# A graph network's first loop: ScalarE alone reads h from PSUM, GpSimd makes half of each row, and the order of the nodes is worked out in eight pieces

## The chip, the cores and the metric

The kernel runs on one core of a Trainium2 chip. Its time is the device time of one execution in microseconds (us), and lower is better. The core has five engines that each work through a queue of their own in order: PE (TensorE, matrix products into PSUM), DVE (VectorE), ACT (ScalarE), POOL (GpSimd) and SP (SyncE, which here only issues transfers). ACT and POOL issue transfers too, from the same queue as their arithmetic. An engine that waits for a semaphore holds up everything behind it in its queue.

## The reference

Four graph layers run one after the other on x, of shape 8 x 2048 x 64 (batch, nodes, features), each followed by a residual and a layer norm. The change lies in the first. Cut to what it touches:

```python
h = x @ W                                            # 8 x 2048 x 64
s = leaky_relu(h @ a_node, 0.2)
alpha = softmax(where(H.T > 0, s[:, None, :], NEG))  # over the nodes, for each of 64 hyperedges
agg = einsum('ben,bnf->bef', alpha, h)               # a weighted mean of h for each hyperedge
beta = sigmoid((h @ a_gn)[:, None, :] + (agg @ a_ge)[:, :, None])
all_he = beta[..., None] * h[:, None] + (1 - beta[..., None]) * agg[:, :, None]
# per node: elu(all_he), weighted over the hyperedges that the node belongs to
```

H says which node belongs to which of the 64 hyperedges; most nodes belong to few. The rest of the layer multiplies by the 2048 x 2048 matrix adj, as do the three layers after it.

## The kernel before

The 2048 nodes stand in NT = 16 groups of 128, one node of a group on each partition, and the loop over t (lines 597 to 645) takes one group per pass. In a pass PE makes h and the two scores h·a_node and h·a_gn for all 8 batches, four products into the PSUM tile ph (L600; two such tiles). DVE clips the scores into seen (L611) and makes the leaky ReLU lr (L618); ACT takes Exp of both (L616 into the row st, L622 into ex). From ph in PSUM, DVE then makes two things: the row st, (h + 1) times the first Exp, in two halves of 4 batches (L625), and ex, h times the second Exp (L629). PE adds ex into the sums of the hyperedges, pagg, with the mask m_n as weights (L637); this is called the gather here. POOL copies the group's slot numbers to the row's end (L614). A row tile holds two passes, there are three such tiles, and after every odd pass ACT issues the store of a pair to hs_hbm (L635, 584 KB).

Meanwhile SP loads x for eight passes ahead (L460). POOL loads blocks of adj (L211); five of them are paced by the loop: `behind` (L482) copies one number of seen so that the load's issue waits for that pass. In passes 9 and 11, `parts` splits a block of x into a high part (ACT, L167) and a low part (POOL, L168).

Later stages take the nodes in order of the number of their hyperedges. Their ranks are worked out ahead of the loop, from L503 to L532. `place`, called in pass 9, turns ranks into the table `order`: DVE finds each rank's tile and row (L558 to L567), two tables of matches (L568 to L575), and one large table ohq of 128 x 2048 comparisons (L578); PE multiplies them (L582, into po) and DVE writes order (L587, L589).

After the loop PE begins the products with adj (ug, L172), POOL fetches the stored rows in the new order (`fetch_rows`, L275) and then the rest of adj, and DVE works out the hyperedges' means from pagg (L674 to L681) and their scores. Products stand in a written order, and `fill` sets pieces of the adj products between the other steps. The tile framework orders instructions that are not pinned with `keep_in_program_order`, and it adds the waits.

Of the kernel before, what the change touches and what calls it, by code (L numbers as in the profile page):

```python
# [30 lines left out]
F32 = mybir.dt.float32  # L31
F32R = mybir.dt.float32r
BF16 = mybir.dt.bfloat16
# [3 lines left out]
AF = mybir.ActivationFunctionType  # L37
ALU = mybir.AluOpType
AX = mybir.AxisListType
# [17 lines left out]
def tile_gnn_fast(  # L57
# [24 lines left out]
    nc = tc.nc  # L82
    B, N, F = out.shape
    E = h_nt.shape[2]
# [14 lines left out]
    def cols(c, n=C):  # L99
        return slice(c * n, (c + 1) * n)  # L100
# [70 lines left out]
    def mm(*args, **kw):  # L171
        tc.keep_in_program_order(nc.tensor.matmul(*args, **kw))  # L172
# [166 lines left out]
    def parts(p, c):  # L339
        part[c] = split(va, xc.pop((p, c)), f"v{c}", 1, [P, JT, P], nc.gpsimd, p == 0)  # L340
# [94 lines left out]
    with tc.tile_pool(name="pa_ps", bufs=1, space=PSUM) as pps:  # L435
# [10 lines left out]
        m_n = pa.tile([P, NT, E], F32, name="m_n")  # L446
        nc.sync.dma_start(m_n, h_nt)

        m_en = pa.tile([P, 2 * HROW], F32, tag="st", name="m_en", bufs=3)[:, 0:2 * C]
        nc.scalar.dma_start(m_en, h_e2)  # L450
        xt = {}

        def fetch_xt(t):
# [86 lines left out]
        pcm = pph.tile([P, 2, C], F32, tag="ph", name="pcm", bufs=2)  # L540
        pcm = pcm.rearrange("p k (t e) -> p (k t) e", e=E)
        mt = so.tile([P, 2 * C], BF16, name="mt")
        nc.vector.tensor_scalar(mt, m_en, 0.0, None, op0=ALU.is_gt)
        for t in range(NT // 2):
            for k in range(2):
                r = slice(k * E, (k + 1) * E)
# [3 lines left out]
        slot = pa.tile([P, NT, E], BF16, name="slot")  # L550
        nc.vector.tensor_tensor(slot, pcm, m_n, ALU.mult)

        def place():

            tl = so.tile([P, NT], F32, name="tl")
            ge = so.tile([P, NT, NT], F32, name="ge")
            tc.keep_in_program_order(
                nc.vector.tensor_scalar(over[:, 0:NT], iota[:, 0:NT], float(P), -0.5, op0=ALU.mult, op1=ALU.add)  # L558
            )
            wide = [P, NT, NT]  # L560
            nc.vector.tensor_tensor(
                ge, rank[:, :, None].to_broadcast(wide), over[:, None, 0:NT].to_broadcast(wide), ALU.is_gt
            )
            nc.vector.tensor_reduce(tl, ge, AX.X, ALU.add)
            nc.vector.tensor_scalar(tl, tl, -1.0, None, op0=ALU.add)
            q = so.tile([P, NT], F32, name="q")
            nc.vector.scalar_tensor_tensor(q, tl, -float(P), rank, op0=ALU.mult, op1=ALU.add)  # L567
            nc.vector.tensor_tensor(  # L568
                ge, tl[:, :, None].to_broadcast(wide), iota[:, None, 0:NT].to_broadcast(wide), ALU.is_equal
            )  # L570
            val = so.tile([P, NT, 2, NT], BF16, name="val")
            nc.vector.tensor_tensor(
                val[:, :, 0, :], ge, iota[:, 0:NT, None].to_broadcast(wide), ALU.mult
            )
            nc.vector.tensor_scalar(val[:, :, 1, :], ge, row, None, op0=ALU.mult)  # L575
            po = pps.tile([P, 2, NT], F32, tag="sm", name="po", bufs=2)
            ohq = so.tile([P, NT, P], BF16, name="ohq")
            nc.vector.tensor_tensor(  # L578
                ohq, q[:, :, None].to_broadcast([P, NT, P]), iota[:, None, :].to_broadcast([P, NT, P]), ALU.is_equal
            )  # L580
            for t in range(NT):
                nc.tensor.matmul(  # L582
                    po.rearrange("p i t -> p (i t)"), lhsT=ohq[:, t, :],
                    rhs=val[:, t].rearrange("p i t -> p (i t)"), start=t == 0, stop=t == NT - 1,
                )
            olo = so.tile([P, NT], F32, name="olo")
            nc.vector.tensor_copy(olo, po[:, 1, :])  # L587

            nc.vector.scalar_tensor_tensor(order, olo, float(NT), po[:, 0, :], op0=ALU.mult, op1=ALU.add)  # L589
            so_scope.close()  # L590


        seen = pa.tile([P, NT, B, 2], F32, name="seen")

        pagg = pps.tile([P, C], F32, tag="agg", name="pagg", bufs=1)
        G = B // 2
        for t in range(NT):
            ph = pph.tile([P, 2, C], F32, tag="ph", name="ph", bufs=2)
            for p in range(NP):
                nc.tensor.matmul(  # L600
                    ph[:, p // 2, (p % 2) * 2 * (F + 2):(p % 2 + 1) * 2 * (F + 2)], lhsT=xt[t][:, p, :],
                    rhs=bd66.rearrange("p b f -> p (b f)"), start=True, stop=True,
                )
            fetch_xt(t + 2 * XB)
            hv = ph[:, :, 0:G * (F + 2)].rearrange("p k (g c) -> p k g c", c=F + 2)
            if t % 2 == 0:
                st2 = pa.tile([P, 2, HROW], F32, tag="st", name="st", bufs=3)
            st = st2[:, t % 2]
            ex = pa.tile([P, 2, G, F + 1], F32, tag="ex", name="ex", bufs=2)
            sv = seen[:, t].rearrange("p (k g) c -> p k g c", k=2)  # L610
            nc.vector.tensor_scalar(  # L611
                sv, hv[:, :, :, F:F + 2], CLIP, -CLIP, op0=ALU.min, op1=ALU.max
            )
            nc.gpsimd.tensor_copy(st[:, BF + 8:], slot[:, t, :])  # L614
            e_gn = st[:, BF:BF + 8]
            nc.scalar.activation(e_gn.rearrange("p (k g) -> p k g", k=2), sv[:, :, :, 1], AF.Exp)  # L616
            lr = pa.tile([P, B], F32, tag="lr", name="lr", bufs=2)
            nc.vector.scalar_tensor_tensor(  # L618
                lr, seen[:, t, :, 0], 0.2, seen[:, t, :, 0], op0=ALU.mult, op1=ALU.max
            )  # L620
            tc.keep_in_program_order(
                nc.scalar.activation(ex[:, :, :, F], lr.rearrange("p (k g) -> p k g", k=2), AF.Exp)  # L622
            )
            for k in range(2):
                nc.vector.scalar_tensor_tensor(  # L625
                    st[:, k * G * F:(k + 1) * G * F].rearrange("p (g f) -> p g f", f=F), hv[:, k, :, 0:F], 1.0,
                    e_gn[:, k * G:(k + 1) * G, None].to_broadcast([P, G, F]), op0=ALU.add, op1=ALU.mult,
                )
            nc.vector.tensor_tensor(  # L629
                ex[:, :, :, 0:F], hv[:, :, :, 0:F], ex[:, :, :, F:F + 1].to_broadcast([P, 2, G, F]), ALU.mult  # L630
            )
            if t == 9:
                place()
            if t % 2:
                nc.scalar.dma_start(hs_hbm.rearrange("(p t) c -> p t c", t=NT)[:, t - 1:t + 1, :], st2)  # L635
            for k in range(2):
                nc.tensor.matmul(  # L637
                    pagg[k * E:(k + 1) * E, 0:G * (F + 1)], lhsT=m_n[:, t, :], rhs=ex[:, k].rearrange("p g c -> p (g c)"),
                    start=t == 0, stop=t == NT - 1,
                )  # L640
            if t in paced:
                behind(seen[:, t, 0, 0:1])
                load_adj(paced[t], 0)
            if t in (9, 11):
                parts(0, (t - 9) // 2)
        nc.vector.tensor_reduce(
            wrong[:, 2:3], seen.rearrange("p t b c -> p (t b c)"), AX.X, ALU.max, apply_absolute_value=True
        )
# [1974 lines left out]
```

## Time and profile before

| | us |
|---|---|
| four runs | 1738.89, 1742.17, 1742.26, 1743.68 |
| median | 1742.21 |
| the profiled execution | 1740.05 |
| its span, first to last instruction | 1737.9 |

| engine | busy us | share of the span |
|---|---|---|
| PE | 1658.7 | 95% |
| DVE | 830.2 | 48% |
| ACT | 589.2 | 34% |
| POOL | 573.0 | 33% |

A line of the timeline reads: start and length in us, engine, line of the kernel, operation, output <- inputs, sizes (partitions x elements), how often, and in brackets the idle time before it with what ended it. Several instructions of one kind in a row are one line; its length runs from the first start to the last end. Instructions of one engine overlap by some 0.08 us, so that a start can lie before the end of the one ahead. DMA issues are shown at the engine's queue, as ACTq or SPq. The granted clock is the share of PE's full clock that the chip allowed. Times in the stages are counted from the start of the span.

### The profile page before, as it was taken

The numbers are of one execution on the slowest core, as the hardware profiler recorded it, in microseconds if no ns is written. First come the engines' busy times: TensorE is split into PE (matmuls) and PEld (weight loads), VectorE is DVE, ScalarE is ACT, GpSimd is POOL, SyncE is SP. The second block draws the span as 40 slices with busy tenths as digits, with TensorE's granted clock in tenths as the row PEclk, the third lists the DMA queues.
The fourth block names the chain that finished last, engine by engine and source line by source line (L and its number), as shares of the span: only waits on it lengthen the run. The fifth ranks groups of instructions, "written<-read, shape, count | busy, mean of one in ns | idle before, by whom it ended". The sixth has DMA issues, their size and how long they took to land. (4 is left out here: it accounts for less than half of the span.)

```text
span 1737.9 us, 27994 instructions
## 1 busy us (share of the span) xinstructions
PE 1658.7 (95%) x11196; PEld 1209.5 (70%) x11196; DVE 830.2 (48%) x1547; ACT 589.2 (34%) x1031; POOL 573.0 (33%) x515
## 2 busy tenths in 40 slices
PE   6888899999989999999999999999989999999996
PEld 4667666666664444468788878888767877878775
DVE  7679945678642221210127247777623433433332
ACT  1345633434321211112123267878512222212221
POOL 4578845556534444422023001323310200202001
PEclk9899999999999999999999999999999999999998
DMA  9743344444240000017344367675571111211111
GB/s 342 244 162 125 103 133 139 153 141 145 94 146 6 31 11 20 25 57 291 118 145 125 108 155 157 133 172 123 157 263 45 53 55 43 61 49 43 56 43 38
DMA packets 171181, 195.83 MB, mean 113 GB/s; under 512 B 71537, under 2 KB 116337, under 8 KB 169761
## 3 DMA queue, kind: packets, MB, share of 16 engines
q1 hardware_dynamic: 160096, 154.54, 30.1%
q0 software_dynamic: 8544, 30.68, 5.2%
q10 hardware_dynamic: 2400, 8.72, 1.4%
q8 instruction: 90, 1.47, 0.4%
q14 instruction: 51, 0.41, 0.1%
HBM read 126.72 MB, written 67.17 MB: 112 GB/s over the span
## 5 line engine op out<-in xcount | busy, mean ns | idle before, releaser
L172 PE MATMUL ua<-pt,xn 128*128 128x512 f32 x512 | 230.2, 592 | 1.4 <-DVE pt L1150 1.4
L172 PEld LDWEIGHTS ua<-pt,xn 128*128 128x128 f32 x512 | 96.9, 190 | 111.1 <-issue 104.0
L1514 DVE COPY w_half<-pw 128x512 f32<-128x512 f32 x160 | 109.8, 706 | 85.7 <-PE pw L172 85.0
L1510 ACT COPY w_half<-pw 128x1024 f32<-128x1024 f32 x128 | 129.8, 1014 | 56.8 <-PE pw L172 56.7
L172 PE MATMUL py<-w_half,xg 128*32 128x128 f32 x4096 | 141.8, 279 | 1.4 <-issue 1.4
L172 PE MATMUL u<-adj,v0h 128*128 128x512 f32 x384 | 134.4, 427 | 1.1 <-ACT h L1818 1.1
L172 PE MATMUL u<-adj_more,v2h 128*128 128x512 f32 x384 | 126.2, 407 | 0.0
L172 PE MATMUL u<-adj_more,v2l 128*128 128x512 f32 x384 | 124.5, 401 | 0.0
L172 PE MATMUL u<-adj,v0l 128*128 128x512 f32 x384 | 124.5, 402 | 0.0
L172 PEld LDWEIGHTS py<-w_half,xg 128*32 128x32 f32 x4096 | 111.1, 138 | 18.7 <-issue 1.8
L1156 POOL TENSOR_TENSOR acc<-acc,pt 128x512 f32<-128x512 f32 x60 | 76.4, 1274 | 104.3 <-DVE pt L1150 103.7
L172 PE MATMUL pw<-est,wst 64*128 64x256 f32 x1024 | 110.1, 318 | 0.4 <-ACT w_half L1510 0.4
L1150 DVE TENSOR_SCALAR pt<-pt 128x512 f32<-128x512 f32 x64 | 29.6, 463 | 152.9 <-ACT pt L1149 152.7
L172 PEld LDWEIGHTS pw<-est,wst 64*128 64x128 f32 x1024 | 82.6, 184 | 25.1 <-ACT w_half L1510 16.7
L1727 ACT CAST ar<-fcav 128x512 fp32r<-128x512 f32 x64 | 39.5, 618 | 166.2 <-DMA fcav<-in_adj_t 165.3
L1149 ACT ACTIVATE pt<-s 128x512 f32<-128x512 f32 x64 | 38.0, 598 | 164.7 <-PE s L172 164.7
L172 PE MATMUL u<-adj,v1h 128*128 128x512 f32 x288 | 93.7, 403 | 0.0
L172 PE MATMUL u<-adj_more,v3h 128*128 128x512 f32 x288 | 93.4, 403 | 0.0
L172 PE MATMUL u<-adj_more,v3l 128*128 128x512 f32 x288 | 93.3, 399 | 0.0
L1728 DVE SCALAR_TENSOR_TENSOR ar<-fcav,ar 128x512 f32<-128x512 f32 x64 | 44.6, 697 | 100.2 <-ACT ar L1727 100.2
L172 PE MATMUL u<-adj,v1l 128*128 128x512 f32 x288 | 92.0, 397 | 0.0
L1699 POOL TENSOR_TENSOR x<-x,rows 128x512 f32<-128x512 f32 x16 | 22.6, 1438 | 210.3 <-PE pt L175 128.5
(406 smaller groups left out, 3274.8 us busy)
## 6 DMA issues: line engine op xcount, KB each, us to landing
fcav<-in_adj_t SPq DMA_DIRECT2D x64, 256.0 KB, 2.9
u_hbm<-ut SPq DMA_DIRECT2D x48, 256.0 KB, 3.3
xg<-u_hbm SPq DMA_DIRECT2D x24, 512.0 KB, 6.9
adj<-in_adj_t POOLq DMA_DIRECT2D x16, 512.0 KB, 8.1
adj_more<-in_adj_t POOLq DMA_DIRECT2D x16, 512.0 KB, 9.2
adj_hbm<-adj_more SPq DMA_DIRECT2D x16, 512.0 KB, 6.4
x_hbm<-r SPq DMA_DIRECT2D x28, 256.0 KB, 2.6
hs_hbm<-st ACTq DMA_DIRECT2D x8, 584.0 KB, 3.5
```

Of the source, the lines that this page charges most:

```text
L172: tc.keep_in_program_order(nc.tensor.matmul(*args, **kw))
L1149: nc.scalar.activation(pt, s, AF.Exp)
L1150: nc.vector.tensor_scalar(pt, pt, 1.0, None, op0=ALU.max)
L1156: nc.gpsimd.tensor_tensor(accs[c], accs[c], pt, ALU.add)
L1510: pin(nc.scalar.copy(dst, pw.rearrange("p j o n -> p n (j o)")))
L1514: pin(copy(dst[:, :, 2 * j:2 * j + 2], bank.rearrange("p o n -> p n o")))
L1699: nc.gpsimd.tensor_tensor(xs, xs, b2.to_broadcast([P, JT, P]), ALU.add)
L1727: nc.scalar.copy(ar, seen_a)
L1728: nc.vector.scalar_tensor_tensor(ar.bitcast(F32), seen_a, 1.0, ar.bitcast(F32), op0=ALU.mult, op1=ALU.not_equal, accum_out=left[:, t, k:k ...
```

## The change

ACT copies h and the scores from PSUM to a new SBUF tile hv (two of them), and writes h + 1 of the second four batches straight into the row with an Identity and a bias. DVE's clip, its half of the row and ex now read hv. POOL multiplies the second half of the row in place by the first Exp. A row tile holds one pass, there are four, and ACT issues a store in every pass (292 KB). The gather of a pass is issued after h of the next. `place` is cut into eight pieces: DVE's steps after passes 4 to 9 (ohq in quarters), PE's product after pass 11, the writing of order after pass 13. Nearly all of the loop's instructions are pinned to the written order. The mask m_en comes in two loads and is compared in two halves. Outside the loop and its preparations one thing differs: of the steps on the hyperedges' means, DVE takes both halves of the ELU (L680, L681) ahead of where it took them, and ACT its copy het.

```diff
-        m_en = pa.tile([P, 2 * HROW], F32, tag="st", name="m_en", bufs=3)[:, 0:2 * C]
-        nc.scalar.dma_start(m_en, h_e2)
+        m_en = [pa.tile([P, HROW], F32, tag="st", name="m_en", bufs=4)[:, 0:C] for _ in range(2)]
+        for i in range(2):
+            nc.scalar.dma_start(m_en[i], h_e2[:, cols(i)])
...
-        nc.vector.tensor_scalar(mt, m_en, 0.0, None, op0=ALU.is_gt)
+        for i in range(2):
+            nc.vector.tensor_scalar(mt[:, cols(i)], m_en[i], 0.0, None, op0=ALU.is_gt)
...
+        def row_columns(i):
+            r, quarter = slice(i * NT // 4, (i + 1) * NT // 4), [P, NT // 4, P]
+            hold(nc.vector.tensor_tensor(
+                ohq[:, r, :], q[:, r, None].to_broadcast(quarter), iota[:, None, :].to_broadcast(quarter),
+                ALU.is_equal,
+            ))
...
+        placing = {4: find_tile, 5: tile_columns, 11: turn_order, 13: write_order}
+        for i in range(4):
+            placing[6 + i] = lambda i=i: row_columns(i)
...
+        def gather(t):
+            ex = exs.pop(t)
+            for k in range(2):
+                mm(pagg[k * E:(k + 1) * E, 0:G * (F + 1)], lhsT=m_n[:, t, :], ...)
...
             fetch_xt(t + 2 * XB)
-            hv = ph[:, :, 0:G * (F + 2)].rearrange("p k (g c) -> p k g c", c=F + 2)
-            if t % 2 == 0:
-                st2 = pa.tile([P, 2, HROW], F32, tag="st", name="st", bufs=3)
-            st = st2[:, t % 2]
+            hv = pa.tile([P, 2, G, F + 2], F32, tag="hv", name="hv", bufs=2)
+            hold(nc.scalar.copy(hv.rearrange("p k g c -> p k (g c)"), ph[:, :, 0:G * (F + 2)]))
+            st = pa.tile([P, HROW], F32, tag="st", name="st", bufs=4)
+            rest = st[:, G * F:BF].rearrange("p (g f) -> p g f", f=F)
+            hold(nc.scalar.activation(
+                rest, ph[:, 1, 0:G * (F + 2)].rearrange("p (g c) -> p g c", c=F + 2)[:, :, 0:F], AF.Identity, bias=1.0
+            ))
...
-            for k in range(2):
-                nc.vector.scalar_tensor_tensor(
-                    st[:, k * G * F:(k + 1) * G * F].rearrange("p (g f) -> p g f", f=F), hv[:, k, :, 0:F], 1.0,
-                    e_gn[:, k * G:(k + 1) * G, None].to_broadcast([P, G, F]), op0=ALU.add, op1=ALU.mult,
-                )
+            hold(nc.vector.scalar_tensor_tensor(
+                st[:, 0:G * F].rearrange("p (g f) -> p g f", f=F), hv[:, 0, :, 0:F], 1.0,
+                e_gn[:, 0:G, None].to_broadcast([P, G, F]), op0=ALU.add, op1=ALU.mult,
+            ))
+            hold(nc.gpsimd.tensor_tensor(rest, rest, e_gn[:, G:B, None].to_broadcast([P, G, F]), ALU.mult))
...
-            if t == 9:
-                place()
-            if t % 2:
-                nc.scalar.dma_start(hs_hbm.rearrange("(p t) c -> p t c", t=NT)[:, t - 1:t + 1, :], st2)
-            for k in range(2):
-                nc.tensor.matmul(...)          # the gather of this pass
+            if t in placing:
+                placing.pop(t)()
+            if t > 0:
+                gather(t - 1)
+            nc.scalar.dma_start(hs_hbm.rearrange("(p t) c -> p t c", t=NT)[:, t, :], st)
```

## Prediction

> **What bounds the kernel now.** I read the page's slices first: PE is 95% busy, but in the first two of the 40 slices (43 us each) it shows 0 and 6 tenths, and the change lies wholly there. So I cut the trace into stages with the windows view. Its columns are the stretch, its length, busy time (count) of PE, PE loads, DVE, ACT and POOL, the granted clock, the DMA share and GB/s.
>
> ```profile
> 14.42:34.26 19.84, 16.55 (x118) 11.34 (x119) 16.46 (x52) 4.34 (x21) 4.96 (x20) 1.00 1.06 400
> 34.26:40.26 6.00, 2.26 (x28) 1.66 (x28) 5.91 (x16) 0.73 (x3) 4.30 (x5) 0.81 0.73 230
> 40.26:55.33 15.07, 11.79 (x57) 7.44 (x57) 8.60 (x27) 3.52 (x13) 1.97 (x4) 0.73 0.42 157
> 55.33:65.34 10.01, 8.00 (x42) 5.74 (x42) 6.39 (x25) 5.64 (x17) 6.47 (x8) 1.00 0.46 139
> 65.34:75.58 10.24, 9.70 (x30) 8.06 (x30) 6.09 (x18) 3.69 (x14) 7.42 (x10) 0.50 1.05 354
> ```
>
> The loop runs from the first clip (14.42) to the end of the last gather (55.33): 40.9 us. Ten nodes (one pass of the loop over t is a node here) take 19.84, or 1.98 each; then DVE is full for 6.00 us with the order of the nodes; then five nodes take 15.07 at a clock of 0.73. ACT is nearly idle throughout. What DVE does in two nodes shows in its timeline:
>
> ```profile
> 22.52 0.17 DVE L611 TENSOR_SCALAR seen<-ph 128x16 f32<-128x16 f32 x1
> 22.72 0.17 DVE L618 SCALAR_TENSOR_TENSOR lr<-seen 128x8 f32<-128x8 f32 x1
> 22.96 0.76 DVE L625 SCALAR_TENSOR_TENSOR st<-ph,st 128x256 f32<-128x256 f32 x2
> 23.64 0.68 DVE L629 TENSOR_TENSOR ex<-ph,ex 128x512 f32<-128x512 f32 x1
> 24.24 0.16 DVE L611 TENSOR_SCALAR seen<-ph 128x16 f32<-128x16 f32 x1
> ```
>
> DVE runs without a hole: 1.72 us a node here. Before the change DVE is the bound; after it, DVE must share an access with POOL. The later part of the trace shows how that goes (timeline of both, 103 to 108 us and 111 to 115):
>
> ```profile
> 104.05 1.29 POOL L803 TENSOR_TENSOR acc<-acc,y 128x512 f32<-128x512 f32 x1 [1.24 <-DVE y L802]
> 105.02 0.87 DVE L802 TENSOR_TENSOR y<-y,co 128x512 f32<-128x512 f32 x1
> 105.81 0.68 DVE L800 TENSOR_TENSOR acc<-y,co 128x512 f32<-128x512 f32 x1
> 106.03 1.61 POOL L803 TENSOR_TENSOR acc<-acc,y 128x512 f32<-128x512 f32 x1 [0.69 <-DVE y L802]
> ...
> 111.68 2.50 DVE L802 TENSOR_TENSOR y<-y,co 128x512 f32<-128x512 f32 x2
> 111.91 1.73 POOL L168 TENSOR_TENSOR hrl<-hrow,hrh 128x512 fp32r<-128x512 f32 x1
> ```
>
> L802 has both inputs in SBUF. At 105.02 it ends 0.55 after POOL does (105.34), though alone it takes 0.68; at 106.03 POOL ends 1.15 after DVE does (106.49), though alone it takes 1.28. So the two exclude each other, and whoever waited saves 0.13 of its own time. At 111.68 the second L802 ends at 114.18, 0.55 after POOL (113.64): POOL was waiting and went ahead of a product queued on DVE. L625 and L629 read ph in PSUM today and showed none of this; after the change both read hv in SBUF. A clip from SBUF is caught too: the 128x2 L731 took 0.94, not 0.16, beside a POOL difference.
>
> ```profile
> 62.37 1.29 POOL L168 TENSOR_TENSOR v3l<-xc,v3h 128x512 fp32r<-128x512 f32 x1
> 62.76 0.94 DVE L731 TENSOR_SCALAR wrong<-wrong 128x2 f32<-128x2 f32 x1
> ```
>
> Last, a store issued by ACT holds that engine (ACT's timeline; the product waited for ended at 41.45):
>
> ```profile
> 41.61 0.33 ACTq L635 DMA_DIRECT2D hs_hbm<-st  x1
> 41.98 0.62 ACT L167 CAST v1h<-xc 128x512 fp32r<-128x512 f32 x1 [1.00 <-DVE st L625]
> ```
>
> So 0.16 from the release to the issue, then 0.33 + 0.04 until ACT works on.
>
> **The change, part by part.**
>
> The new cycle. In the order of the changed program ACT does, for each node: copy of h, Identity+1, first Exp, second Exp, store of the row, and only then the next copy. The store is now in every node and waits for POOL's product; behind that wait stands the next node's copy, and behind it all of DVE's work. One node, from the start of its copy:
> copy 128x528: 0.60 (L414, 128x512 from PSUM, 0.586, and 0.84 ns per further element from L1510) → hand-over 0.04 → clip 0.17 → 0.04 → Exp 0.21: 1.06. DVE's half of the row starts 0.04 later and takes 0.42 (L704, SBUF alone, 128x256, 0.43): 1.52. POOL hears of the Exp some 0.13 later (15.55 to 15.68 in the trace), so it comes second and waits. Its product isn't in the trace; the nearest rows are broadcast products 128x512 (L972 and L1593, 1.04 undisturbed) and plain ones (L1156 1.26, L220 128x128 0.46). From the last two: 0.19 fixed and 2.1 ns an element, 0.73 for 256; with 0.19 and 1.04 for 512: 0.61. I take 0.61, its own kind. Less 0.13: end at 2.00. Then 0.16 + 0.33 + 0.04: 2.53 us a node, against 1.98. A plain 0.73 gives 2.65; no blocking gives 1.06 + 0.13 + 0.61 + 0.53 = 2.33.
>
> The Trainium skill (GPSIMD Engine Reference, section 3.1 Elementwise) speaks against this move: a two-input operation there costs about 2.6 cycles an element at 1.2 GHz, twice the Vector engine's. By that 256 elements would be 0.55 plus the fixed part, an estimate of 0.74, and the loop 2 us longer than my sum; the broadcast rows above are cheaper, and I go by them.
>
> What is covered. Identity+1 (0.37, L1116) ends at 0.89, before the first Exp does. The second Exp lies beside DVE's half row. DVE's weighting of h (0.55 after POOL's end) is over at 2.55; the next clip wants DVE at 2.53 + 0.64 = 3.17, so DVE has 0.70 free (0.08 of it overlap). PE: gather 0.66 and the next-but-one h 1.17 after 2.55 end at 4.43, two cycles are 5.06: 0.63 to spare, at full clock. POOL with a pacing copy and a load: 0.24 + 0.48 + 0.20 + 0.27 + 0.54 = 1.73, under 2.53, so those loads keep their place. The mask in two loads and two compares costs one 0.45 issue ahead of anything that waits, and 0.1 of DVE, under PE's first h (the first clip waited for PE 0.31). Freed DVE time (0.33 a node) is worth nothing now. Sixteen stores for eight: eight more issues, all counted in the cycle.
>
> The eight pieces. find_tile: 0.16+0.41+0.42+0.17+0.17 with hand-overs, 1.37, less 0.70: 0.67. tile_columns: 1.16 - 0.70 = 0.46. A quarter of ohq: 0.68 (from 2.28 for 2048 and 1.04 ns an element), less overlap 0.60, under 0.70: nothing, were DVE not that idle 0.6 each. turn_order (0.59 of PE) fits PE's 0.63; write_order (0.3) fits. The hole in PE at 36 to 39 us goes, and the low clock after it.
>
> The casts of x in nodes 9 and 11 used to lie in idle ACT. Now 0.62 - 0.09 = 0.53 each is in ACT's cycle, and POOL's differences (1.27) that follow block the next clip, as L731 was: some 0.72 each. Together 2.50.
>
> Sum of the loop. 14.42 + 15 x 2.53 + tail (2.55 + 0.05 + 0.66) = 55.63; plus 0.67 + 0.46 + 2.50 = 59.26. That is 3.9 later than 55.33.
>
> What follows. The rows are fetched by POOL when the last store has landed. It is issued at 56.00 + 2.16 = 58.16 against 54.18; it has half the bytes, and 256 KB landed in 2.7 where 584 KB took 3.5, so 0.6 back: 3.4 later. On the other chain, from the last gather, the two he steps of DVE move ahead of the reduction: 0.7 back, 3.2 later. The later one counts: POOL's row fetch, differences and adj loads stand in one queue behind it, and instruction orders of all engines are otherwise as before. Slow nodes (3.0 to 3.25 us) leave PE busy for 1.83 of them; I add 0.4 for a stretch at half clock, about one node at the 2.94 worked out below (2.94 - 2.53). Total +3.8 us: 1743.85 beside the profiled 1740.05 (span 1737.9 and 2.15 around it), and 1746.0 beside the median 1742.21, which the profiled one lies 2.2 under. The Trainium skill (TensorE: Matmul & The Clock Gate, HAM oscillation) lets the clock fall only after idle gaps over some 3.4 us; by that the 0.4 is nothing, but in the trace it is 0.57 from 48 to 52 us, where PE's longest gap just before was 1.76 us.
>
> **The rivals.**
> (1) Not slower: the pair isn't contended by these broadcast forms. A node is 2.33, the tail 2.83, the pieces 0.45 + 0.23, the casts 1.06: 53.9. The store is 1.1 earlier and lands 0.6 sooner: -1.7, 1740.5. It decides where a node is under 2.30. For it: short broadcast forms aren't in the trace beside POOL. Against: every long pair is.
> (2) Slower: four row buffers. A row is stored 2.16 into its node and its buffer wanted 0.51 into the fourth node after: 8.5 us. The view of waits has POOL 10.5 us behind stores, and stores of 19.46 and 21.94 freed their buffers at 27.05 and 30.66: 7.6 and 8.7. Now they are half as large; were it 10, two rounds cost 1.5 each: 1749.
> (3) Half clock in the whole loop: PE needs 1.14 + 2.13, two nodes 2.55 + 0.05 + 3.27 = 5.87, a node 2.94: +6.6 over the sum, 1752. Against: PE would be busy 72% at 2.53.
> (4) The delay isn't carried: DMA is full from 66 to 76 (share 1.05) and the adj loads of that stage might absorb most: about +1, 1743.2. Against: those loads start behind the fetch.
>
> **How the numbers follow.** Main case 0.50 (1746.0, give or take 1.5), (1) 0.17, (2) 0.13, (3) 0.07, (4) 0.13. 0.2% is 3.5 us, about what a measurement of this kernel can tell from no change: 1738.7 to 1745.7. Slower: 0.31 of the main case, (2), (3): 0.51. Faster: two fifths of (1) and a trace of (4): 0.08. Same: 0.41. The range, 1740 to 1751, takes in the product at 0.73 (+1.9 over the sum) with waits for stores above, and (1) below.
>
> **What would show it.** Right: starts of the copies 2.5 apart, each behind a store that waited for POOL; POOL's 128x256 product about 0.8 long, half of it blocked, and ex 1.1 long; copies over 3 us apart at nodes 4 to 5 and about 10 and 12; last gather near 59; clock 1.00 through the loop. Wrong: copies 2.3 or less apart; ACT or POOL behind landings of stores; a clock under 1 before node 12; a last gather before 56.

## The result, and the profile after

The changed kernel takes 1744.07 us (median of 39 runs, 1739.66 to 1749.26), the one before 1741.28 beside it (62 runs, 1735.57 to 1747.59). The ratio is 1.0016, with a 95% interval of 1.001 to 1.0022: 2.8 us slower, between 1.7 and 3.8. Timed once more, on another occasion (11 runs), it was 1.0026, 1.0014 to 1.0039. The forecast was 3.8 us slower. The profiled execution after has a span of 1741.4 us, 3.5 over the one before.

The stages by the windows view, cut at copies of h and at the last gather (columns as before):

```profile
14.97:24.54 9.57, 6.16 (x44) 4.20 (x43) 7.00 (x16) 5.03 (x16) 6.45 (x10) 1.00 1.08 398
24.54:41.03 16.49, 10.54 (x72) 7.02 (x72) 14.85 (x36) 7.77 (x24) 9.50 (x20) 1.00 0.91 315
41.03:53.30 12.27, 7.80 (x64) 5.42 (x64) 9.34 (x18) 6.15 (x18) 6.58 (x12) 0.96 0.58 183
53.30:60.59 7.29, 5.40 (x21) 2.78 (x21) 4.27 (x12) 3.65 (x10) 1.60 (x3) 0.50 0.33 125
```

The first line is four passes, 2.39 each. The second is the six passes with DVE's pieces; those with a quarter of ohq take 2.55 to 2.57 from copy to copy, and DVE is 14.85 busy of 16.49 because the pieces lie here. The third is four passes and the two casts. The fourth is the last two passes at half clock. A plain pass, without a piece and without a cast, is 2.47 there (50.83 to 53.30 below). The loop ends with the last gather at 60.59 instead of 55.33, 5.3 later, and the last store is issued at 58.88 instead of 54.18, 4.7 later.

Two passes side by side, the fourth and the fifth, and two copies of later passes, from the timeline of DVE, POOL and ACT of the changed kernel:

```profile
23.24 0.43 DVE L647 SCALAR_TENSOR_TENSOR st<-hv,st 128x256 f32<-128x256 f32 x1
23.29 0.85 POOL L651 TENSOR_TENSOR st<-st 128x256 f32<-128x256 f32 x1 [0.91 <-ACT st L640]
23.58 1.10 DVE L652 TENSOR_TENSOR ex<-hv,ex 128x512 f32<-128x512 f32 x1
24.17 0.33 ACTq L660 DMA_DIRECT2D hs_hbm<-st  x1
24.54 0.60 ACT L628 COPY hv<-ph 128x528 f32<-128x528 f32 x1 [1.12 <-POOL st L651]
25.67 0.61 POOL L651 TENSOR_TENSOR st<-st 128x256 f32<-128x256 f32 x1 [0.17 <-ACT st L640]
25.68 0.88 DVE L647 SCALAR_TENSOR_TENSOR st<-hv,st 128x256 f32<-128x256 f32 x1
26.48 0.68 DVE L652 TENSOR_TENSOR ex<-hv,ex 128x512 f32<-128x512 f32 x1
...
50.83 0.60 ACT L628 COPY hv<-ph 128x528 f32<-128x528 f32 x1 [1.22 <-POOL st L646]
53.30 0.60 ACT L628 COPY hv<-ph 128x528 f32<-128x528 f32 x1 [1.22 <-PE ph L172]
```

This is the pattern that answers to L802 and L803 in the profile before. In the fourth pass DVE takes its half row first, alone in 0.43; POOL's product stands 0.85 long, and ends at 24.14; ACT issues the store 0.03 later and only then can the copy of the next pass run (24.54). DVE's ex is 1.10 long because POOL had been waiting and went ahead of it. In the fifth pass the two have changed places: POOL's product, 0.01 ahead, runs alone in 0.61, and DVE's half row of 0.43 is 0.88 long. That order then stays to the end of the loop, and a plain pass is 2.47 instead of 2.39, because the store now waits for DVE. A quarter of ohq adds 0.09 to that: it keeps DVE from the next clip.

The casts and POOL's differences, from the same timeline:

```profile
41.03 0.62 ACT L167 CAST v0h<-xc 128x512 fp32r<-128x512 f32 x1 [1.21 <-POOL seen_x L483]
41.56 0.59 ACT L628 COPY hv<-ph 128x528 f32<-128x528 f32 x1
41.74 1.26 POOL L168 TENSOR_TENSOR v0l<-xc,v0h 128x512 fp32r<-128x512 f32 x1 [0.59 <-ACT v0h L167]
42.18 0.86 DVE L636 TENSOR_SCALAR seen<-hv 128x16 f32<-128x16 f32 x1 [0.39 <-ACT hv L628]
```

The cast pushes the copy back by 0.53 (41.03 to 41.56); then the 128x16 clip, 0.17 alone, takes 0.86 beside POOL's difference. And the end of the loop, ACT and POOL:

```profile
55.41 0.33 ACTq L660 DMA_DIRECT2D hs_hbm<-st  x1
56.78 0.60 ACT L628 COPY hv<-ph 128x528 f32<-128x528 f32 x1 [2.21 <-PE ph L172]
58.88 0.33 ACTq L660 DMA_DIRECT2D hs_hbm<-st  x1
61.86 1.07 POOL L275 DMA_INDIRECT hrow<-hs_hbm,order  x1 [3.35 <-DVE agg L698]
```

The same store and fetch in the kernel before:

```profile
54.18 0.33 ACTq L635 DMA_DIRECT2D hs_hbm<-st  x1
58.54 1.31 POOL L275 DMA_INDIRECT hrow<-hs_hbm,order  x1 [14.60 <-DVE he L681]
```

In the changed kernel the last copy waits 1 us longer than those ahead of it, and for PE: the granted clock fell to half at 52.30, and this pass's h took 2.1 instead of 1.2. The fetch of the rows starts at 61.86, 3.3 later than before (58.54). The view names DVE's agg (ended at 61.47) as its releaser, but by the DMA packets the last store's bytes were over at 60.62, and 1.24 lies from there to the fetch; before, they were over at 57.18 and the fetch 1.36 later. In all the profiles of this study it starts 1.21 to 1.37 after the last store's bytes, while the view names DVE's agg, he, tab or sc; so I take the store to be what it waits for. Behind the fetch the shift stays: POOL's first accumulation of a product (acc<-acc,y) stands at 81.91 for 78.44, 3.5 later, and the span ends 3.5 later.

### The profile page after: what moved, and what is told of

Read it like the earlier page. It is cut to its first block, busy times and chain, and to the rows that moved or that the text cites. A ratio compares the mean times of both kernels' runs of the same rounds, so it can differ in the third digit from the quotient of the medians.

```text
span 1741.4 us, 28042 instructions
## 1 busy us (share of the span) xinstructions
PE 1659.5 (95%) x11196; PEld 1208.5 (69%) x11196; DVE 841.5 (48%) x1535; ACT 602.7 (35%) x1063; POOL 585.9 (34%) x531
## 5 line engine op out<-in xcount | busy, mean ns | idle before, releaser
L172 PE MATMUL ua<-pt,xn 128*128 128x512 f32 x512 | 230.2, 592 | 1.4 <-DVE pt L1171 1.4
L172 PEld LDWEIGHTS ua<-pt,xn 128*128 128x128 f32 x512 | 96.9, 190 | 111.1 <-issue 104.2
L172 PE MATMUL py<-w_half,xg 128*32 128x128 f32 x4096 | 141.8, 279 | 1.4 <-issue 1.4
L172 PE MATMUL u<-adj,v0h 128*128 128x512 f32 x384 | 134.4, 428 | 1.1 <-ACT h L1839 1.1
L172 PE MATMUL u<-adj_more,v2h 128*128 128x512 f32 x384 | 126.2, 407 | 0.0
L172 PE MATMUL u<-adj,v0l 128*128 128x512 f32 x384 | 124.5, 402 | 0.0
L172 PE MATMUL u<-adj_more,v2l 128*128 128x512 f32 x384 | 124.3, 400 | 0.0
L172 PEld LDWEIGHTS py<-w_half,xg 128*32 128x32 f32 x4096 | 111.1, 138 | 18.8 <-issue 1.8
L172 PE MATMUL pw<-est,wst 64*128 64x256 f32 x1024 | 110.0, 317 | 0.5 <-ACT w_half L1531 0.4
L172 PEld LDWEIGHTS pw<-est,wst 64*128 64x128 f32 x1024 | 82.4, 184 | 25.2 <-ACT w_half L1531 16.8
L172 PE MATMUL u<-adj_more,v3l 128*128 128x512 f32 x288 | 94.3, 403 | 1.6 <-DVE v3l L168 1.6
L172 PE MATMUL u<-adj_more,v3h 128*128 128x512 f32 x288 | 93.9, 404 | 0.0
L172 PE MATMUL u<-adj,v1h 128*128 128x512 f32 x288 | 93.7, 403 | 0.0
L172 PE MATMUL u<-adj,v1l 128*128 128x512 f32 x288 | 92.0, 397 | 0.0
```

## The experiments

All times are against the kernel before, timed beside it. A plain pass is one without a piece of `place` and without a cast. "Fetch" is the start of POOL's first row fetch in the profile, 58.54 before and 61.86 after the change.

| kernel | plain pass | fetch | ratio, 95% interval | us by the ratio |
|---|---|---|---|---|
| the change | 2.39, then 2.47 | 61.86 | 1.0016 (1.001 to 1.0022) | +2.8 |
| store one pass later | 2.3 | 59.66 | 1.0009 (0.9995 to 1.0023) | +1.6 |
| half row from PSUM | 2.14 | 56.34 | 1.0002 (0.999 to 1.0015) | +0.3 |
| both | 2.1 | 55.61 | 0.9983 (0.997 to 0.9996) | -3.0 |
| pieces only | 2.4 in the mean | 55.08 | 0.9989 (0.9976 to 1.0001) | -1.9 |
| undivided row | 2.2 and waits | 58.22 | 0.9988 (0.9977 to 0.9999) | -2.1 |
| mask and slots in another order | 2.39 | 59.94 | 1.0012 (1.0003 to 1.0022) | +2.1 |
| both, mask behind, gather two later | 1.6 to 2.3, one of 7.3 | 55.44 | 0.9987 (0.9976 to 0.9999) | -2.3 |
| both, mask behind | 2.1 | 54.97 | 0.9971 (0.9957 to 0.9985) | -5.1 |
| copy done twice | 3.0 to 3.1 | 68.38 | 1.0051 (1.003 to 1.0071) | +8.9 |

**The store one pass later.** Is the store's wait for POOL, with the next copy behind it, what paces the loop?

```diff
+            hold(second Exp)
+            if t > 0:
+                store_row(t - 1, last_st)      # ACT: store of the row of the pass before
...
-            nc.scalar.dma_start(hs_hbm...[:, t, :], st)
+            last_st = st
```

> The changed kernel, but the store of a pass is issued one pass later, behind that pass's second Exp, so that no copy of h stands behind a wait for POOL's product. Theory A (a node is the chain copy, clip, Exp, contended product, store issue on ACT): with the store off the chain the next bound is DVE with its contended half row, clip 0.17 + hand-overs 0.3 + half row 0.88 + ex 0.68, so copies 2.0 us apart instead of 2.4 to 2.55, and the pieces now in full (1.4, 1.1, 0.7 four times) as DVE is full; last store issued near 54 instead of 58.9, the whole 4 to 5 us under the changed kernel and about 2 under the one before. Theory B (ACT's copying or POOL's product sets the node, not the place of the store): copies stay 2.4 or more apart and the time within 1 us of the changed kernel. Theory C (the loop's delay is not carried to the end): copies 2.0 apart but the time within 1.5 us of the changed kernel.

The fetch came 2.2 sooner, so the store was on the chain, though the two profiles differ in their spells at half clock too (52.30 there, 45.69 to 49.10 here). The time is only some 1.2 under the changed kernel's, less than the interval of 2.4 to each side. And passes did not fall to 2.0: they alternate between 1.8 and 2.6 at first, run at 2.55 while the pieces fill DVE, and at 2.3 at the end. There the copy waits for PE ("ACT hv L632 <- PE ph L172"), and PE for ex: a gather stands ahead of the next h, so two passes cost gather and h (0.62 + 1.17 + 0.05) and the way from a copy to the end of ex (2.75), 4.6 together. The prediction had this loop of PE as slack ("4.43, two cycles are 5.06"); it is the next bound, and I had left it out of this expectation. Theory A holds for the chain, and its figure for the next bound was wrong.

**DVE's half row from PSUM.** Is it the pair in SBUF on both engines that costs?

```diff
-                st[:, 0:G * F]..., hv[:, 0, :, 0:F], 1.0,
+                st[:, 0:G * F]..., ph[:, 0, 0:G * (F + 2)]...[:, :, 0:F], 1.0,
```

> The changed kernel, but DVE's half of the row reads h from PSUM as before the change, not from the copy, so that it has one wide input in SBUF less. Theory A (DVE's half row and POOL's product exclude each other because both read a pair in SBUF): product 0.61 and half row 0.43 side by side, store issued 1.76 after the copy's start, copies 2.13 apart (2.3 in the four passes with a quarter of ohq, as DVE is then full), the loop 5 us shorter than the changed kernel's and the time 4 to 5 us under it, about 1.5 under the one before. Theory B (they exclude each other whatever DVE reads, or the product's own length sets the node): copies stay 2.4 to 2.55 apart, time within 0.7 us of the changed kernel.

The timeline of DVE, POOL and ACT in a late pass of this kernel:

```profile
50.59 0.61 POOL L652 TENSOR_TENSOR st<-st 128x256 f32<-128x256 f32 x1 [0.88 <-ACT st L640]
50.60 0.42 DVE L647 SCALAR_TENSOR_TENSOR st<-ph,st 128x256 f32<-128x256 f32 x1
50.94 0.81 DVE L653 TENSOR_TENSOR ex<-hv,ex 128x512 f32<-128x512 f32 x1
51.23 0.33 ACTq L661 DMA_DIRECT2D hs_hbm<-st  x1
51.60 0.60 ACT L628 COPY hv<-ph 128x528 f32<-128x528 f32 x1 [0.88 <-PE ph L172]
```

The same 256 columns, the same output, one input moved from SBUF to PSUM: product and half row now run side by side at 0.61 and 0.42, and passes are 2.14 to 2.16 apart in all of the loop but for the pieces and casts (2.13 expected). Only ex, which still reads a pair in SBUF, waits the rest of the product (0.81 for 0.68). Theory A is shown: the exclusion hangs on where DVE reads. The Trainium skill (SBUF — State Buffer, Who interferes with whom) has the rule: outside the modes that use both ports, a DVE instruction with at most one input in SBUF does not contend with GpSimd; one with two contends with a GpSimd instruction that reads SBUF; and the order of issue decides who waits. The half row and ex agree on each count. The clip beside POOL's difference does not fall under the first part: it reads hv alone, and yet took 0.86 for 0.17. The page counts tensor_scalar, which the clip is, among the operations that can enter those modes; that it did so here no run shows. The exclusion cost 0.25 a pass in the first four and 0.33 to 0.36 in the later ones without a cast. The fetch is 5.5 us sooner, of which 1.0 is the half clock in the changed kernel's last copy, absent here. The time fell only by some 2.5 of these, with an interval 2.2 to each side; this profile ran 2.0 ahead of the one before until 120 us and then met spells of half clock at 130.68, 154.57 and 840.65 that the profile before doesn't have (the last cost 1.6).

**Both edits,** the two diffs above together.

> Both edits at once: the store one pass later, and DVE's half row from PSUM. Theory A: neither the store nor the shared access is on the chain, so PE (gather 0.66 and h 1.17), DVE (1.5 and the pieces) and the transfers (some 800 KB a pass up to pass 10 at about 400 GB/s, 2.0 us) set the pace: copies 1.9 to 2.1 apart, last store issued near 49 to 50, the time 7 to 9 us under the changed kernel and 4 to 6 under the one before. If the two costs were one and the same, it is no faster than the better of the two single edits.

Fetch at 55.61, 6.3 sooner than in the changed kernel; the time is 3.0 us under the kernel before, where 4 to 6 were expected. The two costs add up, though not in full, for PE's loop sets the pace. Its timeline:

```profile
47.25 0.66 PE L172 MATMUL pagg<-ex,m_n 128*64 128x260 f32 x4 [0.84 <-DVE ex L659]
47.84 1.17 PE L172 MATMUL ph<-firsts,xt 128*128 128x132 f32 x8
48.94 0.66 PE L172 MATMUL pagg<-ex,m_n 128*64 128x260 f32 x4
49.53 1.17 PE L172 MATMUL ph<-firsts,xt 128*128 128x132 f32 x8
```

A wait for ex in every second pass, then two gathers and two h without a hole: 4.2 us for two passes.

**The pieces only.** The kernel before, with this part of the change:

```diff
-            if t == 9:
-                place()
+            if t in placing:          # the eight pieces, as in the change
+                placing.pop(t)()
```

> The kernel before, with the order of the nodes worked out in the eight pieces and nothing else of the change. If the 6.0 us in which DVE was full with that order, and the five passes at a lowered clock behind it (3.0 us each), were the loss of the loop before, the passes now stay at 1.98 us, plus the pieces' DVE time of 5.1 us spread over passes 4 to 9: last gather near 52 instead of 55.3, the time 3 us under the one before. If the clock falls all the same, or the last passes wait for something else (x, stores), the last gather stays within 1 us of 55.3 and so does the time. Either way it tells how much of the changed kernel's result the pieces give and how much the new division of the row costs.

DVE's solid 6.00 us is gone, the last gather ends at 52.63 (52 expected) and the fetch is 3.5 sooner. But passes do not stay at 1.98: they take 2.4 in the mean (first clips from 14.37 to 49.96) and 2.6 at the end, where PE waits for ex and DVE for h. So this part of the change is worth about 3.5 us at the fetch of this profile; the rest of the change takes it back, and 3.3 more. In the time a gain is not sure: 1.9 us, between 4.2 less and 0.2 more.

**The undivided row.** The kernel of the pieces alone, with the gather moved as in the change:

```diff
-            for k in range(2):
-                nc.tensor.matmul(...)          # the gather of this pass
+            exs[t] = ex
+            if t > 0:
+                gather(t - 1)
```

> All of the change but the new division of the row: the row and ex made by DVE from PSUM and pairs of rows stored, as before, with the order in eight pieces and the gather one pass later. If the new division is what costs, this is the fastest so far but for the last kernel of this call: DVE 1.72 us a pass and 5.1 us for the pieces, 32.6 us in all, with PE's chain (gather 0.66, h 1.17, then ex) no longer in its way: last gather near 49 to 50, the time 4 to 6 us under the kernel before. If PE's order is still what paces it, the last gather stays near 52.6 as with the pieces alone and the time 2 us under the one before.

The forecast failed. The last gather ends at 55.77, and PE's timeline shows why:

```profile
41.27 0.81 PE L172 MATMUL pagg<-ex,m_n 128*64 128x260 f32 x4 [2.85 <-DVE ex L649]
42.00 2.13 PE L172 MATMUL ph<-firsts,xt 128*128 128x132 f32 x8
```

DVE's steps are not pinned here: they are queued as two clips, then the rows of two passes, so PE waits long for ex. The clock was at half from 41.64 to 45.05, and h took 2.13. So it does not tell what the gather's new place is worth by itself. The runs lie a little under the kernel before although the profile's fetch is only 0.3 sooner; a profile is one execution.

**Mask behind the count, slots on DVE.** Two misses of the prediction, told apart in one trace.

```diff
+        keep_in_program_order(deg reduce, gtb copy, both mask compares, gt product)   # in this order
...
-            hold(nc.gpsimd.tensor_copy(st[:, BF + 8:], slot[:, t, :]))
+            hold(nc.vector.tensor_copy(st[:, BF + 8:], slot[:, t, :]))    # ahead of the clip
```

> The changed kernel with two edits whose marks in the trace are apart. First, the two mask compares are pinned behind the count of each node's hyperedges, in the hole where DVE waits for PE, so that the count does not stand behind the second mask load. Expected: the count starts where the compare of the first mask ends, 1.2 to 1.7 us sooner, and the first clip comes near 14.2 instead of 15.6; if x is late instead, it stays at 15.6. Second, DVE copies the slot numbers into the row ahead of its clip, so that the wait for a row buffer's store lies on that copy and not on DVE's half row. Theory A (from pass 4 on POOL's product goes first because DVE's half row has one more wait in front of it there, the one for the buffer): half row 0.43 and product 0.84 in all passes, and plain passes of 2.40 us instead of 2.55. Theory B (the order changes in pass 4 for another reason): 0.88 and 0.61 again from pass 4, passes of 2.55. Together with A the last store is issued some 2.5 to 3 us sooner than in the changed kernel, time 2 to 3 us under it.

DVE's start, first of the kernel before, then of the changed one (timeline):

```profile
5.93 0.69 DVE L501 TENSOR_SCALAR m_n<-m_n 128x1024 f32<-128x1024 f32 x1
7.13 0.69 DVE L543 TENSOR_SCALAR mt<-m_en 128x1024 bf16<-128x1024 f32 x1 [0.50 <-DMA m_en<-in_h_e]
7.74 1.21 DVE L503 TENSOR_REDUCE deg<-m_n 128x16 f32<-128x1024 f32 x1
```

```profile
6.81 0.69 DVE L502 TENSOR_SCALAR m_n<-m_n 128x1024 f32<-128x1024 f32 x1
7.89 0.43 DVE L545 TENSOR_SCALAR mt<-m_en 128x512 bf16<-128x512 f32 x1 [0.40 <-DMA m_en<-in_h_e]
8.23 1.21 DVE L504 TENSOR_REDUCE deg<-m_n 128x16 f32<-128x1024 f32 x1
```

The count deg needs no m_en, yet stands behind its compare in DVE's queue; with the mask in two loads the second lands later, and count, ranks and the loop's start (14.97, the first copy, for 14.42, the first clip) all shift by some 0.5. Pinned behind the count, the compares fill DVE's wait for PE, the count starts at 6.68 and the first clip at 14.13 instead of 15.60. And the tenth pass of this kernel (DVE, POOL):

```profile
39.18 0.43 DVE L647 SCALAR_TENSOR_TENSOR st<-hv,st 128x256 f32<-128x256 f32 x1
39.22 0.85 POOL L651 TENSOR_TENSOR st<-st 128x256 f32<-128x256 f32 x1 [1.66 <-ACT st L641]
```

Half row first, in every pass but the last; plain passes are 2.38 to 2.40 to the end, and the one with a quarter of ohq that neither a cast nor half clock touches is 2.46. Theory A is shown: in the changed kernel DVE's half row carries, from the fifth pass on, a second wait, for the store that frees its row buffer. The changed kernel's trace has it as a separate semaphore instruction ahead of the half row (L647; none in the first four passes, one in each of the other twelve, none in this kernel), which then starts 0.09 after the Exp instead of 0.03, while POOL's product starts at 0.08: 0.06 us turn the order round and cost some 0.09 a pass. (The Trainium skill, Perfetto Trace Analysis, Identifying Dependency Chains, says that an instruction that waits for several engines may have such instructions put ahead of it.) The fetch is 1.9 sooner than in the changed kernel, less than the 2.5 to 3 expected, as the clock was at half from 30.35 to 37.18 in this profile (one pass of 3.28 from clip to clip). The time is 2.1 over the kernel before, only some 0.7 under the changed kernel's.

**Gather two passes later,** on top of the late store, the half row from PSUM and the mask compares behind the count.

```diff
-            if t > 0:
-                gather(t - 1)
+            if t > 1:
+                gather(t - 2)      # ex in three buffers
```

> The changed kernel with what the runs so far point to: the store one pass later, DVE's half row from PSUM, the mask compares behind the count, and the gather two passes later (three ex buffers; the mask's comparisons share memory with ohq), so that h does not stand behind ex in PE's queue. With the late store and the PSUM reading alone, two passes took 4.15 us, all of it the loop ex, gather 0.66, h 1.17, copy to ex 2.30. If that loop is the bound, passes fall to 1.85 to 2.0 (PE's 1.83, transfers up to pass 10), first clip near 14.2, last store near 47 to 48 instead of 58.9, row fetch near 50 to 51 instead of 61.9, time 6 to 8 us under the kernel before if the rows behind can take it. If the transfers (x, stores, adj) set the pace instead, passes stay at 2.1 or more and the gain over the two edits alone is the start's 1.4 us only.

The early passes do fall to 1.6, and then ACT meets what the prediction's second rival was about. Its timeline:

```profile
20.79 0.60 ACT L632 COPY hv<-ph 128x528 f32<-128x528 f32 x1 [0.21 <-issue]
25.73 0.38 ACT L635 ACTIVATE st<-ph 128x256 f32<-128x256 f32 x1 [4.35 <-DMA hs_hbm<-st]
```

The fifth pass waits 4.35 for the store of the first to land, so that buffer, not PE, paces the loop up to there. So the expected 6 to 8 us did not come: fetch at 55.44, and 2.3 under the kernel before.

**The same with the gather one pass later,** as in the change: the late store, the half row from PSUM, the mask compares behind the count, by the diffs above.

> The store one pass later and DVE's half row from PSUM, as before, and the mask compares behind the count; the gather stays one pass later. With the gather two passes later the first passes took 1.6 us and the fifth then waited 4.3 us for its row buffer's store; at two passes in 4.15 us that wait should be smaller. If the 1.4 us that the loop starts sooner are kept: last store near 51, row fetch near 54.2 instead of 55.6, time 1 to 1.5 us under the same kernel without the mask's edit, 4 to 5 under the kernel before. If the row buffers (four, each waiting for its store while the transfers are at their full rate) set the loop's pace, the sooner start is lost in the fifth pass and row fetch and time stay at 55.6 and 3 us under.

Fetch at 54.97, 0.6 of the 1.2 of the sooner start kept; 0.9971 (0.9957 to 0.9985), 5.1 us under the kernel before. It is faster than both kernels of this study, by the interval at least 2.6 us under the one before.

**The copy done twice.** Does a delay of the loop reach the end?

```diff
             hold(nc.scalar.copy(hv..., ph...))
+            hold(nc.scalar.copy(hv..., ph...))
```

> The changed kernel with ACT's copy of h done twice in every pass, on the chain that paces the loop: 0.5 to 0.56 us more a pass (a second copy overlaps the first by some 0.08), 8 to 9 us in 16 passes, less what the passes with a piece or a cast hide (up to 1.5). It is a test, on a larger scale than the change's own 3 us, of how much of a delay in the loop reaches the end. Theory A (row fetch, differences and adj loads stand in one queue behind the last store, so a delay goes through whole): row fetch 7 to 9 us later than in the changed kernel, and the time later by the same, 1750.5 to 1752.5. Theory B (the stage behind, whose transfers are at their full rate, absorbs much of it): row fetch as late, but the time only 2 to 5 us later, 1746 to 1749.

Passes 3.0 to 3.1, fetch 6.5 later than in the changed kernel (the pieces now hide, and the last pass does not wait for PE), POOL's first accumulation 6.5 later as well (88.44 for 81.91): the stage in between, which the prediction's fourth rival named, takes nothing back. The time is 8.9 over the kernel before (5.2 to 12.4), so 6.1 over the changed one by its first timing, and 4.4 by its second, below. Of the delay, then, all reaches 90 us; how much of it reaches the end is known only to some 3.5 us, and theory B, with 2 to 5, is not excluded by the times.

**Small products to keep the clock up.** Four 128x128 products a pass into a spare PSUM tile, from the eighth pass, and in a second kernel from the thirteenth.

```diff
+            if t >= 7:      # second kernel: t >= 12
+                for _ in range(4):
+                    mm(warm, lhsT=ident, rhs=ident, start=True, stop=True)
```

> The changed kernel with four small products (128x128, result not used) on PE in every pass from the eighth on, some 0.45 us a pass in PE's idle time. In the changed kernel the clock fell to half from 52.3 to 62.5, the copy of the last pass then waited for PE (3.48 us after the copy ahead of it instead of 2.47) and the last gather took 1.1 instead of 0.66. If the fall comes from PE being busy too little, the clock now stays at 1.00 through the loop's end, the last gather ends near 59.2 instead of 60.6, the last store is issued near 57.9, and the time is 1 to 1.5 us under the changed kernel. If the clock falls whatever PE does in its gaps, the extra products make the end later: last gather 60.6 to 61.5, time the same or up to 1 us over.

> The changed kernel with the four small products on PE only in the passes from the thirteenth on (from about 48 us), where the clock fell in the changed kernel. With them in every pass from the eighth on, the clock stayed at 1.00 through the loop and the last gather ended 0.7 us sooner, yet the time was 4.9 us longer than the changed kernel's, and nothing in the first 120 us shows more than 1 us of it. If the longer time came from something that the extra products do to the rest of the program, it should shrink with their number: clock 1.00 to the loop's end, last gather near 59.5, time 1 us under to 1 us over the changed kernel run beside it. If it came from the change of PSUM buffers that the extra tile brings (it is the same here), the time stays 4 to 5 us over the changed kernel. If it was mostly scatter of a few runs, both kernels stand within 1 us.

The products kept PE busy for 1.16 us a pass, not the 0.45 expected. The first kernel shows no fall of the clock before 69 us and the last gather at 59.93 for 60.59, as expected of a clock that falls when PE is too idle. It is one trace; the second kernel had a spell at 45.18 and none later in the loop, and the changed kernel profiled again (below) had its own at 46.60 and 60.25. Against the idea stands the kernel with the copy done twice: by the windows view PE is busy there for 26.81 of 50.52 us of the loop (53%), less than the 23.59 of 37.33 (63%) of the changed kernel up to its fall, and yet its clock is 1.00 up to 65.5. So what makes the clock fall in the loop stays open. What was not expected is the time: 1.0044 (1.0028 to 1.006) and 1.0093 (1.0076 to 1.0109), 7.7 and 16 us over the kernel before. Up to 1050 us the second kernel's DVE runs as far behind the kernel before as the changed one (4.0 and 3.9); from there to 1290 it falls back by 15 more. The view of waits in 1060 to 1285 us of that kernel:

```profile
DVE w_half L1539 <- PE pw L172: 58.1, 91, 3.7
PEld py L172 <- issue: 8.1, 8, 1.8
PEld pw L172 <- issue: 7.8, 27, 3.0
```

PE itself waits there for nothing that the profile shows ("issue"): 8.1 us ahead of the loads for py, where the same view of the changed kernel has 1.8, and one wait of 3.0 ahead of pw, where it has none over 0.2. DVE waits 58.1 for PE instead of 44.1. Two spells at half clock of 3.41 us lie in this stage (1151.10 and 1239.85) that the changed kernel's profile does not have there; at the 1.6 us that one cost in the kernel with the half row from PSUM, they would make some 3 of the 15. In both kernels the 16 KB transfers of the instruction queue come mostly every 4 to 8 us in this stage and every 25 to 50 elsewhere; that extra instructions shift where PE's code falls into these pieces is my explanation, argued and not shown. The products also need a PSUM tile of their own, and no run tells its part from theirs. For the first kernel the loss is spread over several places and has no explanation. Theories of the clock can't be weighed by these two times.

**The changed kernel again.** 

> The changed kernel itself, unaltered, timed beside the one before it on the same chip and in the same rounds as the last warm kernel, so that the two can be compared directly: 2.8 us over the kernel before (1.7 to 3.8) if the difference does not depend on chip and hour.

1.0026 (1.0014 to 1.0039), 4.5 us over the one before; fetch at 61.27. Both intervals hold the forecast of 3.8.

## Why the prediction was right, step by step

The mechanism was right: a chain of copy, clip, Exp, the contended half rows and the store sets the pass, the loop ends later, and the fetch of the rows with it. Its details were right for the first four passes; after them DVE and POOL have changed places. That the sum came so close at the fetch (3.3 later for 3.4) is in part luck, for five misses of 0.5 to 1.2 us cancel in it.

- **Start.** I called the mask's two halves covered. They cost 0.5: the second compare stands ahead of the count. I had asked what hides the extra issue and not what is queued behind the second load's compare.
- **Cycle.** 2.53 was forecast; it is 2.39 in four passes and 2.47 in the plain ones after, so the fifteen cycles of the sum are some 1.2 us shorter. Copy to Exp 1.05 (1.06), product 0.61 (0.61 forecast from the broadcast rows; the plain rows' 0.73, and the estimate of 0.74 from the Trainium skill, GPSIMD Engine Reference, 3.1 Elementwise, were too long), half row 0.43 (0.42). Three terms were off. From the release to the issue it is 0.03 behind POOL and 0.09 behind DVE, not 0.16. POOL starts 0.08 after the Exp, not 0.13 (the rows at 15.55 and 15.68 are a wait for DVE's clip, not for an Exp), so DVE leads by 0.05 and not by 0.09. And DVE first, POOL blocked, as I had it, holds for four passes only, and with it the signs "product about 0.8 long" and "ex 1.1 long". With POOL first the store waits for DVE's 0.88.
- **Pieces.** Against a plain pass of 2.47, find_tile cost 0.89 in the two passes that it touches (3.26 and 2.57; 0.67 forecast), tile_columns 0.51 (0.46), and each quarter 0.09, 0.35 in all (nothing forecast): 0.6 us more. The store of find_tile's pass was issued late, at 27.43, 0.87 after its half row was done; a semaphore instruction stands right ahead of it, but what that waited for is not shown. It cost nothing: in the first kernel with small products this store is issued in time (26.58), and the two passes take 2.47 and 3.36, the same 5.83 together, as find_tile then holds the next clip.
- **Casts.** 2.4 for 2.50: four passes of 3.08, 3.14, 2.99, 3.14, each longer by 0.53 for the cast or by about 0.67 for the blocked clip, the first by a quarter of ohq as well.
- **Clock.** I gave 0.4 to a stretch of half clock "about one node". In the profile it cost 1.0 in the last copy and 0.5 in the last gather, and a second profile of the same kernel has other spells. The size of this term was not to be had from one trace, and the sign "clock 1.00 through the loop" did not come. That the clock falls after passes in which PE never idles for over 2 us was seen again (at 46.60 in the second profile, 1.56 the longest gap just before), so that the rule that the prediction quoted from the Trainium skill (TensorE: Matmul & The Clock Gate, HAM oscillation), a fall only after idle gaps over some 3.4 us, does not describe this loop: the longest gap ahead of the fall at 52.30 was 1.94.
- **Last store.** 58.16 forecast, 58.88 measured: later by 0.55 for the start, 0.6 for the pieces and 1.0 for the clock, sooner by 1.2 for the cycle and 0.1 for the casts. The landing: 0.6 sooner forecast, 1.26 measured (last bytes 1.74 after the issue instead of 3.00). So the fetch is 3.3 later for 3.4.
- **Carried.** 3.3 at the fetch, 3.5 at 100 us, 2.8 and 4.5 us by the two ratios. The copy done twice shows it on a larger scale up to 90 us. It is not exact: in the second profile of the changed kernel the fetch is 2.7 later than before, but POOL's first accumulation 2.1 (80.53 for 78.44) and its fourth 1.4 (88.14 for 86.70). That profile has 6.8 us at half clock between 60 and 76 us, for 10.2 in the kernel before; that this makes the difference is not shown.
- **Rivals.** (1) lost: the broadcast forms are contended; without contention a pass is 2.14, not the 2.33 that it gave. (2) did not occur in this kernel beyond one slot copy that waited 0.55, but it is real at 1.6 us a pass. (3) did not occur. (4) lost: with the copy done twice, the stage that it named gave nothing back.
- **A slip.** The page's first two slices show PE at 6 and 8 tenths, not at 0 and 6; nothing in the sum rests on it.

## What to carry to other kernels

An engine that issues a store carries the wait of that store for everyone behind it in its queue: put the issue behind the next pass's first steps. If GpSimd shares a loop with the Vector engine, look at where the Vector engine's inputs lie: leave one of them in PSUM rather than copy it to SBUF, for here both then ran at full speed (2.14 for 2.47 us a plain pass). After each bound that you take away ask for the next one before you forecast: here, behind the store, stood PE's order (2.1 to 2.3 us a pass), and behind that the row buffers.

## What the runs showed of the hardware that I had not expected

- Who comes first at the shared access is settled by hundredths of a microsecond, and can change in the middle of a loop when one engine gets a second semaphore to wait for: 0.43 and 0.85 became 0.88 and 0.61.
- A store issued by ACT that waited for POOL left 0.03 us after the product's end, for 0.09 behind DVE.
- Sixteen small products on PE at 50 us, with a PSUM tile of their own, were followed by a stage at 1050 to 1290 us that took 15 us longer, with PE waiting for its own issue; the cause is open.
- Every spell at half clock lasted a multiple of 3.41 us (3.41, 6.83, 10.24), except at the program's end, and the spells differ between kernels in stages that the edit does not touch; with one lasting 3.41 us costing some 1.6, this may be much of the scatter of some 10 us between runs; no run here shows it.
